# Another order for the same pieces of a two-layer graph kernel

## The chip, the cores and the metric

The kernel runs on one core of a Trainium2 chip. A core has five instruction queues that run at the same time: TensorE (PE, matrix products, with its weight loads shown as PEld), VectorE (DVE), ScalarE (ACT), GpSimd (POOL) and SyncE (SP, which issues the transfers here). Each works through its own instructions strictly in order and waits for the others by semaphores. The metric is device time in microseconds, lower is better.

## The reference

128 graphs of 128 nodes with 64 features pass two layers, each closed by a residual and a layer norm. In the first, every node j sums a ReLU over its neighbours k; in the second, a two-layer message is summed with the adjacency as weights and goes through a gated update.

```python
# layer 0, per graph: x [128, 64], adj [128, 128]
mask = (adj > 0.0)
h  = relu((x @ W1a)[:, None, :] + (x[:, None, :] - x[None, :, :]) @ W1b + b1)   # [j, k, 192]
hm = einsum('jkh,jk->jh', h, mask)
x  = layernorm(x + hm @ W2 + deg[:, None] * b2)
# layer 1
m   = relu(relu(x @ W1 + b1) @ W2 + b2)
msg = relu(adj @ m)
r, z = sigmoid(...), sigmoid(...)          # of msg @ W_ih and x @ W_hh, with biases
n   = tanh(i_n + r * h_n)
x   = layernorm(x + (1 - z) * n + z * x)
```

## The kernel before

The inner sum of layer 0 is ReLU(u_j + v_k), and ReLU(a) = (a + |a|) / 2, so the kernel sums absolute values over the neighbours. It does not go over all 128 k. The neighbours of a node are ranked in each half of the graph; for rank r a 0/1 matrix `pick` says which k is the r-th neighbour of each j. A product of `pick` with the rows of v (the *gather*, L628) fetches that neighbour's v for all nodes at once. The first eight ranks of each half come from `pick0` (comparisons of `rankT` with a constant, L534); nodes with more neighbours borrow extra rows, and `pick1` (comparisons of `place`) serves those with four more ranks. `own` and `past` (L480, L481) say which extra row belongs to which node: the *row owners* of the title's change, turned by PE (`pq`, L508) into `ownT` (L511).

The graphs are worked on in 32 groups of four. A group has 24 *stretches* (six for each graph: four with `pick0`, two with `pick1`), and a stretch takes two ranks of both halves:

- *seed* (L597, ACT): copy u four times into a PSUM buffer `pv`
- *gather* (L628, PE): 12 products add the picked v, which is held as three bfloat16 pieces `b0`, `b1`, `b2`
- *reduce* (L644, DVE): sum of absolute values of the buffer into `part`

There are three `pv` buffers, so the seed of stretch k+3 waits for the reduce of stretch k. All the rest must find a place between the stretches. To prepare a later group: masks (L428, POOL), ranks (L435, L438), degrees (L443 to L448), counts (L453 to L463, POOL), offsets with own/past, turned, places (L517 to L527), values (u and v: `pu` L544 and L547, `uv` L551), pieces (`b0` L563, `r` L566, `b1` L569, `b2` L572), the picks, over (`pz` L608, `us` L615: u of the extra rows). To finish a group: base (L656), together (sums of `part`, L666 to L673, POOL), sums (`ph` L685 and L686, `hmT` L692), second (`pw`, `y` L305 and the first layer norm L274 to L287, which gives `x1`), turn, message1 to 3 (`pm`, `pn`, `pa`), gates (`pg`, `rz` L366, `rh` L368, `n` L369) and update (tanh L374, four sums, second layer norm, store). All of these steps that use a product share two further PSUM buffers (the pool `ps_w`), taken in turn: a product waits until the result that lay in its buffer two takings before has been read out by ACT or DVE.

The order is written out by hand, as a timetable. Each part is a generator; one entry in its list of times is one step, up to the next `yield`. The times are in units of no meaning beyond their order; a group is `PER` units long, and group g runs the same list shifted by `g * PER`:

```python
for name, times in TIMETABLE.items():
    if g == 0 and name in FIRST:
        times = FIRST[name] + times[len(FIRST[name]) :]
    run = parts[name]()
    for t in times:
        plan.setdefault(g * PER + t, []).append(run)
...
with tc.manual_schedule():
    for t in sorted(plan):
        for run in plan[t]:
            next(run, None)
```

So the sorted times set the order of the instructions on every queue, and which of the two `ps_w` buffers a step gets. Nothing else is decided by them: what an instruction waits for is its operands and its buffer. In the steady state the work of one group's length contains stretches of group g, finishing of groups g-1 to g-5 and preparation of groups g+1 to g+3.

Of the kernel before, what the change touches and what calls it, by code (L numbers as in the profile page):

```python
# [26 lines left out]
EPS = 1e-5  # L27


PER = 768  # L30
TIMETABLE = {
    "load": (-1520,), "masks": (-559,), "ranks": (-122, -122), "degrees": (-402, -367), "turned": (-19, -1),
    "counts": (-114,), "offsets": (-22, -22, 80, 228, 245, 348, 349), "owners": (1039, 1066), "places": (368, 431),
    "pieces": (337, 538, 550, 595), "others": (1085, 1194), "values0": (-55, -50, -37), "values1": (204, 204, 268),
    "pick0": (-44, 50, 88, 133, 133, 137, 251, 419), "pick1": (663, 679, 679, 679), "over0": (578, 602),
    "over2": (1053, 1123), "base0": (693,), "together0": (728, 840, 1185, 1275), "sums0": (1392, 1392, 1405),
    "base1": (708,), "together1": (1189, 1219, 1289, 1289), "base2": (443,), "together2": (1345, 1353, 1370, 1370),
    "sums2": (1443, 1449, 1449), "base3": (717,), "together3": (1408, 1417, 1417, 1417),
    "second": (1425, 1453, 1473, 1502, 1502, 1503), "turn": (1504, 1504), "message1": (1512, 1512),
    "message2": (1534, 1538), "message3": (1539, 1696), "gates": (2002, 2032, 2052, 2068, 2068, 2080),  # L40
    "update": (2201, 2201, 2333, 2396, 2584, 2918, 3390, 3734, 4832),
    "seed": (644, 644, 657, 674, 684, 685, 711, 728, 728, 741, 761, 837, 923, 937, 978, 1149, 1149, 1173, 1203, 1221,
        1271, 1326, 1395, 1397),
    "gather": (661, 661, 681, 681, 686, 708, 730, 730, 737, 748, 767, 940, 1026, 1051, 1110, 1161, 1163, 1189, 1238,
        1317, 1338, 1405, 1405, 1405),
    "reduce": (664, 678, 684, 684, 706, 724, 740, 743, 780, 862, 894, 947, 1119, 1138, 1138, 1192, 1215, 1233, 1263,
        1358, 1358, 1407, 1407, 1407),
}


SETUP = (-8001, -7999, -7610, -7530, -7400, -7380, -700, -690)
FIRST = {
    "load": (-8000, -7998), "masks": (-7580,), "ranks": (-7520, -7515), "degrees": (-7389, -7388), "counts": (-7387,),
    "offsets": (-7372, -7371, -7366, -7366, -7366, -7366, -7365), "turned": (-7359, -7358),
    "values0": (-7375, -7374, -7370), "values1": (-7368, -7364, -7360), "pieces": (-7373, -7363, -7355, -7350),
    "places": (-7357, -7356), "pick0": (-7512, -7512, -7512, -7512, -7365, -7365, -7365, -7365),
    "pick1": (-7352, -7352, -7351, -7351), "over0": (-7349, -7348), "seed": (-7369, -7366, -7361, -7354),
    "gather": (-7367, -7362, -7354, -7351), "reduce": (-7365, -7358, -7353, -7350),
}

@with_exitstack
def adj_resnorm_kernel(  # L80
# [316 lines left out]
    with ExitStack() as fast:  # L397
# [323 lines left out]
        name, g, run = "setup", -1, setup(ps_g, ps_w)  # L721
        for t in SETUP:
            plan.setdefault(t, []).append(run)
        for g in range(ng):
# [9 lines left out]
            if g == ng - 1:  # L734
                plan.setdefault(g * PER + TIMETABLE["reduce"][-1] + 1, []).append(parts["spare"]())
            for name, times in TIMETABLE.items():
# [3 lines left out]
# [3 lines that stand above are left out]
# [126 lines left out]
```

## Time and profile before

| what | value |
|---|---|
| median of 3 runs (lowest to highest) | 1049.1 us (1049.07 to 1049.19) |
| span of the profiled execution (no other time of it is given) | 1047.0 us |
| first reduce of group 0 | 18.82 us |
| reduce 4 of group 0 | 33.08 us |
| `y` (L305) of the first, the 31st and the last group | 64.01, 996.04, 1023.81 us |
| `y` to `y` in an undisturbed middle group | 30.98 us |
| granted TensorE clock, mean | 0.983 (1.00 from 62 to 1000 us) |
| reduces: 768, busy | 699.6 us |
| comparisons: 384, busy | 120.5 us |

The span is the time from the first to the last instruction; the times measured without the profiler are a little longer than it. `y` is the instruction with which a finished group leaves the first layer; it occurs once for each group, so its distance is the length of a group. Busy time counts an instruction's whole length; successive instructions of one engine overlap at their ends, so the distance from start to start is shorter than the length (a reduce is recorded at 949 ns and follows the one before after 865).

### The profile page before, as it was taken

To read this page: it belongs to the slowest core of one execution; us is meant where nothing else is said; L and a number is where in the kernel's file an instruction comes from. 1 tells how busy PE (TensorE), PEld (TensorE's weight loads), DVE (VectorE), ACT (ScalarE), POOL (GpSimd) and SP (SyncE) were. 2 spreads that over 40 slices of the span, in tenths; PEclk is the share of its full clock that TensorE was granted. 3 is DMA by queue.
4 is the path that set the end of the run, shared out by engine and by line. 5 is a ranking of instruction groups with operands and counts; after the bars stand their busy time and mean duration, and the time that the engine had idled before them with its cause. 6 is when DMAs were issued, how large, how long until landed. Compare 5 with 4: busy or idle time off the path is not lost.

```text
span 1047.0 us, 33471 instructions
## 1 busy us (share of the span) xinstructions
PE 952.5 (91%) x13447; PEld 761.0 (73%) x13447; DVE 972.5 (93%) x2202; ACT 943.0 (90%) x1608; POOL 876.6 (84%) x1281
## 2 busy tenths in 40 slices
PE   6798999999999999999999999999999999999984
PEld 3577777777787777777777777777777777777762
DVE  6988999999999999999999999999999999999983
ACT  4789999999999999999999999999999999999971
POOL 2568788889888888988888988988898888898864
PEclk7899999999999999999999999999999999999997
DMA  4000000000000000000000000000000000000000
GB/s 111 1 23 2 23 21 23 28 27 10 19 27 27 27 27 27 3 27 28 26 28 28 4 24 28 27 28 28 24 5 28 27 27 27 27 3 7 7 8 28
DMA packets 21368, 23.95 MB, mean 23 GB/s; under 512 B 4050, under 2 KB 17112, under 8 KB 21208
## 3 DMA queue, kind: packets, MB, share of 16 engines
q1 hardware_dynamic: 21208, 21.76, 7.0%
q8 instruction: 107, 1.75, 0.7%
q14 instruction: 53, 0.43, 0.1%
HBM read 17.55 MB, written 4.19 MB: 21 GB/s over the span
## 4 chain that ended last, share of the span: by engine, by line
PE 31%; DVE 21%; ACT 20%; POOL 20%; issue 7%; DMA 0%; SPq 0%; DVEq 0%; POOLq 0%; ACTq 0%
PE pv L628 12%; ACT pv L597 10%; DVE part L644 10%; PE ph L686 3%; ACT uv L551 3%; POOL part L666 3%; PE pu L544 2%; POOL rs L281 2%; DVE stats L274 2%; DVE pick L534 2%; ACT b L563 2%; PE ph L685 2%; POOL part L670 2%; POOL part L673 2%; POOL r L566 2%
## 5 line engine op out<-in xcount | busy, mean ns | idle before, releaser
L644 DVE TENSOR_REDUCE part<-pv 128x192 f32<-128x768 f32 x768 | 699.6, 949 | 31.6 <-PE pv L628 15.6
L628 PE MATMUL pv<-b,pick 64*128 64x192 bf16 x9216 | 501.6, 244 | 39.1 <-ACT pv L597 34.9
L628 PEld LDWEIGHTS <-pick 64*128 64x128 bf16 x9216 | 385.0, 94 | 123.9 <-issue 94.4
L597 ACT COPY pv<-uv 128x768 f32<-128x768 f32 x512 | 407.5, 804 | 16.6 <-DVE part L644 14.2
L597 ACT COPY pv<-us 128x768 f32<-128x768 f32 x256 | 204.7, 817 | 13.2 <-DVE part L644 13.1
L666 POOL TENSOR_TENSOR part<-part 128x384 f32<-128x384 f32 x128 | 127.8, 998 | 19.7 <-DVE part L644 17.7
L551 ACT COPY uv<-pu 128x512 f32<-128x512 f32 x128 | 75.1, 587 | 27.3 <-PE pu L547 23.1
L544 PE MATMUL pu<-wall,xT 64*128 64x512 f32 x256 | 92.3, 637 | 1.4 <-ACT off L473 1.2
L534 DVE TENSOR_SCALAR pick<-rankT 128x512 bf16<-128x512 bf16 x256 | 88.6, 367 | 1.3 <-ACT rankT L438 1.3
L686 PE MATMUL ph<-ownT,part 128*96 128x128 f32 x512 | 87.6, 273 | 0.2 <-POOL part L673 0.2
L487 POOL CAST own<-own 128x512 f32<-128x512 bf16 x32 | 19.5, 610 | 75.2 <-DVE own L481 69.1
L668 POOL TENSOR_TENSOR part<-part 128x192 f32<-128x192 f32 x128 | 77.3, 604 | 5.1
L572 POOL TENSOR_TENSOR b<-r,b 128x1024 bf16<-128x1024 f32 (+1 forms) x35 | 68.8, 1966 | 12.1 <-ACT b L569 8.9
L670 POOL TENSOR_TENSOR part<-part 128x192 f32<-128x192 f32 x128 | 75.6, 590 | 2.6
L608 PE MATMUL pz<-uv,own 128*128 128x192 f32 x256 | 58.6, 352 | 20.4 <-DVE n L369 12.0
L300 PE MATMUL pw<-w2c,hmT 96*128 96x64 f32 x512 | 75.1, 278 | 0.7 <-ACT hmT L692 0.7
L673 POOL TENSOR_TENSOR part<-part 128x192 f32<-128x192 f32 x128 | 75.5, 590 | 0.0
L300 PEld LDWEIGHTS pw<-w2c,hmT 96*128 96x128 f32 x512 | 69.8, 192 | 6.8 <-issue 4.9
L686 PEld LDWEIGHTS ph<-ownT,part 128*96 128x96 f32 x512 | 70.9, 166 | 1.8 <-POOL part L673 0.7
L685 PE MATMUL ph<-ident,part 128*96 128x128 f32 x256 | 71.0, 277 | 0.8 <-POOL part L670 0.6
L281 POOL TENSOR_TENSOR rs<-ve,nhalf 128x4 f32<-128x4 f32 x64 | 66.7, 1042 | 5.3
L566 POOL TENSOR_TENSOR r<-uv,b 128x1024 f32<-128x1024 f32 x31 | 66.0, 2130 | 0.0
(148 smaller groups left out, 1588.4 us busy)
## 6 DMA issues: line engine op xcount, KB each, us to landing
adjT<-in_adjT_dram SPq DMA_DIRECT2D x32, 256.0 KB, 2.8
xT<-in_xT_dram SPq DMA_DIRECT2D x64, 64.0 KB, 2.6
x<-in_x_dram SPq DMA_DIRECT2D x32, 128.0 KB, 2.4
out_dram<-o SPq DMA_DIRECT2D x32, 128.0 KB, 2.0
wab<-in_w_dram SPq DMA_DIRECT2D x2, 96.0 KB, 2.5
bi<-in_b_ih_dram SPq DMA_DIRECT2D x1, 96.0 KB
bias<-in_b_hh_dram SPq DMA_DIRECT2D x1, 96.0 KB
wx<-in_w_hhT_dram SPq DMA_DIRECT2D x2, 48.0 KB, 3.6
```

The lines of the kernel that those rows point to most:

```text
L300: nc.tensor.matmul(p[:, i, :], s["hmT"][:, i, c, :], w2c[:, c, :], start=c == 0, stop=False)
L534: nc.vector.tensor_scalar(s[name][:, i], s[src], 2.0 * (first + i) - 1.0, None, ALU.is_equal)
L544: nc.tensor.matmul(ps[h], s["xT"][ks, i, :], wall[ks, :], start=True, stop=False)
L551: nc.scalar.copy(uv[:, 2 * h + i, :], ps[h])
L597: nc.scalar.copy(v, src.rearrange("p (c b h) -> p c b h", c=1, b=1).to_broadcast(list(v.shape)))
L628: nc.tensor.matmul(v[:, h, j, :], pick[ks, a + j, i, :], s[f"b{c}"][ks, i, F : F + H], start=False, stop=c == 2, skip_group_check=True,)
L644: nc.vector.tensor_reduce(into, view(s["pv", i, k]).rearrange("p c b h -> p h c b"), AX.XY, ALU.add, apply_absolute_value=True,)
L666: nc.gpsimd.tensor_tensor(f[:, 0:2], f[:, 0:2], f[:, 2:4], ALU.add)
L670: nc.gpsimd.tensor_tensor(f[:, 0], f[:, 0], f[:, no], ALU.subtract)
L673: nc.gpsimd.tensor_tensor(f[:, 0], f[:, 0], f[:, 1], ALU.add)
L685: nc.tensor.transpose(p[:, i, c, :], s["part", i0 + i][:, 0, cs], ident)
L686: nc.tensor.matmul(p[:, i, c, :], s["part1", i0 + i][:, 0, cs], s["ownT"][:, i0 + i, :], start=False, stop=True, skip_group_check=True,)
```

## The change

Only the two timetables, the list `SETUP` and the unit `PER` differ; every instruction is the same, and each queue has as many as before. The whole shift of the numbers (PER ten times as large, a later zero) means nothing; the order that comes out is what counts. Within a group's length, against the stretches:

- copies of u (seed) stand one stretch sooner on ACT relative to small results such as `m1`, `m2` and the first `uv` of values0, which come behind a further copy
- ranks: PE's product from before gather 0 to after gather 4
- row owners (`pq`): from after gather 12 to after gather 10
- message3: from after gather 10 to after gather 13; places before degrees; over0 after sums0 instead of ahead of it
- comparisons on DVE: before, `pick0` between reduce 5 and reduce 14 of the group ahead and `pick1` between reduce 23 and reduce 2; after, they stand behind reduce 14, 17, 20, 22, 23 and 0, `pick0` and `pick1` in mixed order, the last three of `pick0` only after the group's own reduce 0
- the statistics of update (L274): from after reduce 20 to after reduce 4
- `b0` (L563): from after seed 14 to after seed 17; the `base` rows are spread differently
- loads: two groups ahead instead of three
- the first group and the setup have their own order: the first adjacency load goes ahead of the weight loads, the load of group 1 behind all of setup's loads, degrees ahead of ranks, and seeds 4 and 5 ahead of the second group's ranks

```diff
-PER = 768
+PER = 7680
 TIMETABLE = {
-    "load": (-1520,), "masks": (-559,), "ranks": (-122, -122), "degrees": (-402, -367), "turned": (-19, -1),
-    "counts": (-114,), "offsets": (-22, -22, 80, 228, 245, 348, 349), "owners": (1039, 1066), "places": (368, 431),
-    "pieces": (337, 538, 550, 595), "others": (1085, 1194), "values0": (-55, -50, -37), "values1": (204, 204, 268),
-    "pick0": (-44, 50, 88, 133, 133, 137, 251, 419), "pick1": (663, 679, 679, 679), "over0": (578, 602),
+    "load": (-13730,), "masks": (-12008,), "ranks": (-5844, -5844), "degrees": (-10379, -10179),
+    "turned": (-4917, -4474), "counts": (-5544,), "offsets": (-5208, -5187, -4765, -4509, -3829, -3198, -1474),
+    "owners": (3311, 3746), "places": (-2998, -2655), "pieces": (-2359, -1040, -1012, -282), "others": (-2397, -1574),
+    "values0": (-5666, -5639, -5639), "values1": (-3673, -3446, -3378),
+    "pick0": (-2699, -2480, -1412, -657, -89, 643, 704, 916), "pick1": (-1456, -673, -79, 517), "over0": (-597, -272),
...
-    "seed": (644, 644, 657, 674, 684, 685, 711, 728, 728, 741, 761, 837, 923, 937, 978, 1149, 1149, 1173, 1203, 1221,
-        1271, 1326, 1395, 1397),
+    "seed": (-172, -168, 227, 921, 1341, 1368, 2018, 2018, 2445, 2612, 3169, 3460, 4084, 4145, 4425, 4839, 4956,
+        5224, 5461, 5704, 6457, 6732, 6776, 7296),
...
-    "reduce": (664, 678, 684, 684, 706, 724, 740, 743, 780, 862, 894, 947, 1119, 1138, 1138, 1192, 1215, 1233, 1263,
-        1358, 1358, 1407, 1407, 1407),
+    "reduce": (571, 936, 1241, 1588, 1982, 2334, 2334, 2605, 2916, 3415, 3415, 4224, 4224, 4511, 4736, 5225, 5348,
+        5582, 6391, 6623, 6925, 7255, 7423, 7607),
 }
-SETUP = (-8001, -7999, -7610, -7530, -7400, -7380, -700, -690)
+SETUP = (-113105, -109386, -107102, -104025, -100032, -97526, -25206, -11107)
 FIRST = {
-    "load": (-8000, -7998), "masks": (-7580,), "ranks": (-7520, -7515), "degrees": (-7389, -7388), "counts": (-7387,),
+    "load": (-113322, -99309), "masks": (-105433,), "ranks": (-95876, -94299), "degrees": (-101486, -100699),
+    "turned": (-92902, -92053), "counts": (-97744,),
...
```

## The prediction

> **What bounds the kernel now.** I read the page's busy shares first, then the chain of waits inside one middle group, then the timelines of that group on VectorE and GpSimd.
>
> ```profile
> PE 952.5 (91%) x13447; PEld 761.0 (73%) x13447; DVE 972.5 (93%) x2202; ACT 943.0 (90%) x1608; POOL 876.6 (84%) x1281
> ```
>
> No engine stands alone: three are over 90% busy. The first `y` (L305) comes at 64.0 us, the 31st at 996.0, so a group takes 31.07 us on average and 30.98 when nothing disturbs it. These lines of the chain of waits, cut to 590 to 626 us, show one such group from `y` to `y`:
>
> ```profile
> 592.14 0.43 DVE y L305
> ...
> 596.24 0.44 PE pt L312 x2
> ...
> 601.41 1.12 PE pu L544 x3
> 602.53 0.45 PE pu L547
> ...
> 612.17 0.30 DVE rh L368
> ...
> 612.93 0.89 PE pz L608 x4
> ...
> 623.12 0.43 DVE y L305
> ```
>
> The chain changes engine all the time. I cut the group at three VectorE points: `y` at 592.14, the gates' `rh` at 612.17, reduce 21 (stretch 21 of 24) at 615.84, the next `y` at 623.12. The pieces are A 20.03, B 3.67 and C 7.28, together 30.98 us. Next, VectorE's timeline, whose rows are start, length, instruction:
>
> ```profile
> 595.10 0.55 DVE L534 TENSOR_SCALAR pick<-rankT 128x512 bf16<-128x512 bf16 x1
> ...
> 598.27 0.56 DVE L534 TENSOR_SCALAR pick<-rankT 128x512 bf16<-128x512 bf16 x1
> ...
> 601.37 0.68 DVE L534 TENSOR_SCALAR pick<-rankT 128x512 bf16<-128x512 bf16 x3
> ...
> 608.22 3.75 DVE L644 TENSOR_REDUCE part<-pv 128x192 f32<-128x768 f32 x4 [0.42 <-PE pv L628]
> ```
>
> and GpSimd's beside it:
>
> ```profile
> 594.88 0.61 POOL L284 TENSOR_TENSOR yc<-y,mv 128x256 f32<-128x256 f32 x1
> ...
> 598.08 1.50 POOL L428 TENSOR_SCALAR maskT<-adjT 128x512 bf16<-128x512 f32 x1
> ...
> 601.41 0.48 POOL L279 TENSOR_SCALAR ve<-mv 128x4 f32<-128x4 f32 x1
> ```
>
> A comparison (`pick`) holds VectorE for 0.20 us when GpSimd works on 4-element rows (three in 0.68), but 0.47 when a large GpSimd instruction runs beside it (595.10: the next starts at 595.57). I call that a collision, price 0.27. Of twelve comparisons in this group two pay all of it and one (beside the mask's end) half: 0.7 us. None of those that read `place` pays: over 200 to 900 us they take 275 to 292 ns.
>
> **The change part by part.** Steady prices, as start-to-start distances when the engine does not wait: reduce 0.865, copy of u 0.73, 12 gather matmuls 0.60, `y` with its statistics 1.26, update's statistics 0.89, a `past`/`own` pair 0.55, degrees 0.15. From a reduce's start to the copy that reuses its buffer 0.99; copy to gather 0.85; gather to reduce 0.72. Times below count from `y`.
>
> *Piece A, PE's side.* Now update's statistics stand after reduce 4, so reduce 5 starts at 1.26+0.865+0.89 = 3.02, copy 8 at 4.01, gather 8 at 4.86 (`x1` arrives at 4.10, hidden). From there the new order leaves PE no wait. Gather 8 0.60, `pr` 0.33, `pm` 0.63, gathers 9 and 10 1.20, `pq` 0.33 (row owners, now two stretches sooner), `pn` 0.56, gather 11 0.60, `values1` 1.00, gathers 12 and 13 1.18, `pz` 0.87, `pa` 0.68, together 7.98. Gather 14 starts at 12.84 and reduce 14 at 13.56. Here lies the gain: before, `values1` waited for its second buffer and took 1.57 (1.12+0.45 above) instead of 1.00, because message3's result was released a copy too late; owners and message3 now stand where both buffers are free. Copies of u, a stretch sooner against the small results, delay none of them here: `m1` is ready at 7.5 and PE wants it at 7.95. The run goes on with gather 14 0.60, `ps` and `pd` 1.11, gathers 15 and 16 1.16, first gates 0.87, gather 17 0.60, second gates 0.68, and gather 18 starts at 17.86. Reduce 18 could start at 18.6 and `rh` at 19.5: A would win 0.55.
>
> *Piece A, VectorE's side.* Two comparisons now frame degrees after reduce 14, and two follow reduce 17. Reduce 14 ends at 14.43. By GpSimd's new order `x1` ends at 4.1 and the work behind it (0.95 + 1.47 + 1.35 + 0.55 + 0.95 + 0.55 + 0.55 + 0.69 + 0.55 + 0.57 + 0.55 + 0.58 + 0.55 + 0.69 + 0.57) fills it to 15.2, so both collide: 0.48+0.15+0.48, reduce 15 at 15.54, reduce 17 ends at 18.17. `r` (L566, 2.09) starts once the parts after reduce 15 are done, 17.4 to 19.4: two more collisions. Reduce 18 starts at 19.13, `rh` at 20.0: A stays at 20.0, the gain is given back.
>
> *Piece B.* Sums0 goes before over0: the same two jobs. 0.53 (`rh`, `n`) + 0.13 + 1.35 + 0.87 + 0.75 = 3.63: no change. The two comparisons between reduce 20 and 21 take the place of update's statistics (0.89) and are hidden by this; uncovered they cost 0.4 to 0.95.
>
> *Piece C.* VectorE sets it: seven reduces 6.06, and now six comparisons where four stood (before they and their small waits filled the 1.22 left). `pick0.4` pays 0.08, `pick1.2` 0.27 (beside `together3`, released by reduce 21), `pick1.3` falls into a gap, and `pick0.5` to `.7` after reduce 0 run beside `o`, `ub`, `uc`, which reduce 23 releases: 0.81. C is 6.06+1.22+1.16 = 8.45. PE, waiting at sums2 for GpSimd, would allow about 7.3.
>
> [...]
>
> *Other moves.* Pieces' first cast (`b0`) goes three copies later; `b2` then ends about 1.5 before gather 0 wants it; uncovered, up to 2.1 a group. Ranks go from before gather 0 to after gather 4; the first comparison is ten stretches away. The four `base` rows change places on ACT (0.36 each, same sum). GpSimd's counts stand before `ve` and leave it free 1.2 before `mv`. SP loads two groups ahead instead of three and behind a store; landing takes 2.8, the mask has about 5: nothing, uncovered up to 2.8 once, since SP's later loads keep that lead.
>
> *First group.* SP issues the first adjacency load before the weights (0.6 each way), degrees come first, the four early comparisons later. Reduce 0 comes at about 17.5 instead of 18.82. Copies 4 and 5 stood behind the second group's ranks (which wait for a mask until 30.5); now they stand ahead of them. Reduce 4 should start at 30 instead of 33.08: 3 us gained, bounds 0 and 5 (the idle VectorE rows before it). Group 1's load is issued after fourteen weight loads, about 16.5 instead of 6.83; its mask runs at 26 or later.
>
> *Tail.* From the last `y` at 1023.81 to 1047.0 the chain is one group's own and keeps its order: 0, bounds -1.5 and +1.5 (the longest wait in it that another group could set).
>
> Sum: a group 20.0+3.65+8.45 = 32.1, 1.1 more; 30 such groups +33, first group -3, and some groups will hide a little: +27. The span goes from 1047.0 to 1074. The page gives no other time for the profiled execution; the median lies 2.1 above its span, kept as what lies around it: 1076.
>
> **The rivals.**
> *The comparisons do not collide* (faster). If GpSimd's large rows stand elsewhere than I place them, A is 19.5, B 3.65, C 7.3: 30.4 a group, 30 x -0.55 - 3 = -19, 1030. For it: PE's waits for copies (34.9 us in 42 by the list of waits) and the late buffer of `values1` do vanish. Against: reduce 0 to reduce 1 has `o`, `ub`, `uc` beside it by its own release. It decides when fewer than some five of twelve collide on the path.
> *Half of them count.* Collisions in A are hidden behind PE, only C's remain: 19.5+3.65+8.45 = 31.6, or 31.2 with two of the trio free. Total 1052 to 1065. Nothing excludes it; A's two sides differ by 0.5.
> *More waits.* Copies ahead of the small results make ACT sit on a buffer while `uv`, `m1` or hmT are wanted; each costs up to 0.5 a group (ACT's longest steady wait for `values1` is 0.52). One of them makes 32.6 a group and 1095, two make 33.1 and 1110.
>
> **How the numbers follow.** Forecast (1066 to 1088) 0.45; half 0.22; no collisions 0.20; more waits 0.13. The range 1040 to 1094 leaves out about 0.1 below (most of the collision-free case) and 0.1 above. A measurement here can tell 0.2%, about 2 us: faster 0.20, same 0.03 (the half case's lower edge), slower 0.77.
>
> **What would show it.** `y` to `y` of 32.1 in the middle. Comparisons from `place` no longer 284 ns but some near 550, all comparisons together rising from 120 us to about 180. `values1` in 1.0 without a wait. A of 20.0, C near 8.4. Reduce 4 of the first group near 30. I am wrong if C stays near 7.3, or if PE waits inside its run from gather 8 to 18.

## The result, and the profile after

The changed kernel takes 1155.5 us (median of four runs, 1154.3 to 1156.8) against 1049.1 us for the kernel before, measured beside it. The ratio is 1.1009, with a 95% interval of 1.0993 to 1.1025. The profiled execution has a span of 1155.0 us, 108.0 us more than before.

One thing has to be known to read the rows. The timetable of the changed kernel is fifteen lines shorter, so every line number is 15 lower than before: the reduce is L629 (before L644), the gather L613 (L628), the copy of u L582 (L597), the comparison L519 (L534), `own` L466 (L481), `r` L551 (L566), `b2` L557 (L572), `y` L290 (L305), `n` L354 (L369), the parts L651 to L658 (L666 to L673), `ph` L670 and L671 (L685 and L686), `pz` L593 (L608). The experiments keep the line numbers of before, except where it is said.

The first two lines of the changed kernel's page that matter are the busy shares and the granted TensorE clock in forty slices:

```profile
PE 1025.6 (89%) x13446; PEld 816.3 (71%) x13447; DVE 1061.6 (92%) x2202; ACT 958.2 (83%) x1608; POOL 881.2 (76%) x1281
...
PEclk9999999999999989999899998999989999899998
```

VectorE is busy for 89 us more and TensorE for 73 us more, although both have the instructions that they had. So instructions have become longer. The clock line says why for TensorE: it no longer gets its full clock in the middle of the run (mean 0.943; before 0.983, and 1.00 from 62 to 1000 us). For VectorE the groups by line say it, whose last three columns are the busy sum in us, the mean length in ns, and idle time:

```profile
L519 DVE TENSOR_SCALAR pick<-rankT 128x512 bf16<-128x512 bf16 x256 | 123.7, 503 | 0.0
...
L519 DVE TENSOR_SCALAR pick<-place 128x512 bf16<-128x512 bf16 x128 | 85.5, 670 | 0.0
```

The comparisons of `rankT` had a mean of 367 ns, those of `place` 291. Together they rose from 120.5 us to 209.2.

The first `y` comes at 61.68 us (before 64.01), the last at 1133.21, and from there to the end it is 21.8 us (before 23.2). So the ends of the run gained 2.3 and 1.4 us, and the 31 distances between them lost 111.7. The loss is in the steady state. I cut each of the groups 5 to 25 at the three points of the prediction and took the mean. In the table, "blocked" is the length of the comparisons, `past` and `own` of a group over what they take when GpSimd leaves them alone (0.283, 0.245 and 0.351 us), and "half clock" the time in a group in which TensorE was granted half its clock.

| kernel | group | A (`y` to `rh`) | B (`rh` to reduce 21) | C (reduce 21 to `y`) | blocked | half clock |
|---|---|---|---|---|---|---|
| before | 31.00 | 20.03 | 3.67 | 7.30 | 0.70 | 0 |
| after | 34.98 | 21.37 | 5.33 | 8.28 | 4.19 | 4.27 |

The three pieces lost 1.34, 1.66 and 0.98 us. The VectorE timeline of one group in the middle, from `y` to `y`, shows where:

```profile
614.77 0.41 DVE L290 TENSOR_TENSOR y<-pw,t 128x256 f32<-128x256 f32 x1
...
624.30 0.73 DVE L466 SCALAR_TENSOR_TENSOR own<-iota,off,past 128x128 bf16<-128x128 bf16 x1
...
633.08 1.66 DVE L519 TENSOR_SCALAR pick<-place 128x512 bf16<-128x512 bf16 x1
634.66 0.68 DVE L519 TENSOR_SCALAR pick<-rankT 128x512 bf16<-128x512 bf16 x1
...
636.13 0.27 DVE L353 TENSOR_TENSOR rh<-rz,pg 128x128 f32<-128x128 f32 x1
...
641.34 1.82 DVE L629 TENSOR_REDUCE part<-pv 128x192 f32<-128x768 f32 x2 [1.97 <-PE pv L613]
...
645.78 1.31 DVE L519 TENSOR_SCALAR pick<-rankT 128x512 bf16<-128x512 bf16 x3
...
649.61 0.41 DVE L290 TENSOR_TENSOR y<-pw,t 128x256 f32<-128x256 f32 x1
```

and GpSimd's timeline beside it:

```profile
624.29 0.60 POOL L653 TENSOR_TENSOR part<-part 128x192 f32<-128x192 f32 x1
...
632.46 2.13 POOL L551 TENSOR_TENSOR r<-uv,b 128x1024 f32<-128x1024 f32 x1
634.55 0.64 POOL L653 TENSOR_TENSOR part<-part 128x192 f32<-128x192 f32 x1
...
645.97 0.77 POOL L365 TENSOR_TENSOR ub<-ua,rz 128x256 f32<-128x256 f32 x1
```

`pick1.0` starts at 633.08, 0.62 us into `r`, and lasts 1.66 us, until 634.74. `r` ended at 634.59. The next comparison stands beside the addition of 634.55 to 635.19 and ends at 635.34. Two comparisons that need 0.48 us alone have taken 2.2. In A this is the largest single loss; an `own` of 0.73 instead of 0.35 at 624.30 stands beside an addition in the same way, and the three comparisons at 645.78 stand beside `ub` and others in C.

What follows in B is on TensorE. Its timeline in the same group, with the idle time before an instruction and what ended it in brackets:

```profile
634.19 0.67 PE L613 MATMUL pv<-b,pick 64*128 64x192 bf16 x12 [0.34 <-ACT pv L582]
636.87 0.28 PE L670 MATMUL ph<-ident,part 128*96 128x128 f32 x1 [2.01 <-DVE n L354]
...
638.84 1.49 PE L593 MATMUL pz<-uv,own 128*128 128x192 f32 x4
640.26 1.96 PE L613 MATMUL pv<-b,pick 64*128 64x192 bf16 x36
```

sums0 stands ahead of over0 now. Its `ph` needs the `ps_w` buffer of the first gates, which is free when the first `n` has read it. In the kernel before, over0's `pz` had this place and the same wait, only shorter:

```profile
612.93 0.89 PE L608 MATMUL pz<-uv,own 128*128 128x192 f32 x4 [0.38 <-DVE n L369]
```

In both kernels the job behind gather 20 starts about 0.75 us after the first `rh` (612.93 after 612.17, and 636.87 after 636.13). So the order of the two jobs is not what made the difference. TensorE did its gathers in time, and the two comparisons made reduce 18 and the gates late: it has nothing to do for 2.0 us instead of 0.38. The busy time by windows shows what it does then (start and end, length, busy time of PE, PEld, DVE, ACT and POOL with counts, granted clock, DMA share, GB/s):

```profile
634.00:637.00 3.00, 0.80 (x14) 0.60 (x14) 2.93 (x7) 2.48 (x5) 2.92 (x4) 1.00 0.02 5
637.00:640.00 3.00, 3.00 (x16) 2.81 (x15) 2.37 (x5) 1.78 (x4) 1.49 (x2) 0.58 0.00 0
```

After three microseconds with 0.80 us of work the granted clock is 0.58 on average in the next three. The four products of `pz` take 1.49 us instead of the 0.89 of before, gather 21 comes late, and VectorE waits 1.97 us for it: the bracket at 641.34 above. The half-clock stretches last 3.41 us in most groups and 6.83 in every fourth.

### The profile page after: what moved, and what is told of

Its sections match the earlier page's. It is cut to its first block, busy times and chain, and to the rows that moved or that the text cites. A ratio compares the mean times of both kernels' runs of the same rounds, so it can differ in the third digit from the quotient of the medians.

```text
span 1155.0 us, 33471 instructions
## 1 busy us (share of the span) xinstructions
PE 1025.6 (89%) x13446; PEld 816.3 (71%) x13447; DVE 1061.6 (92%) x2202; ACT 958.2 (83%) x1608; POOL 881.2 (76%) x1281
## 3 DMA queue, kind: packets, MB, share of 16 engines
q8 instruction: 107, 1.75, 0.6%
HBM read 17.55 MB, written 4.19 MB: 19 GB/s over the span
## 5 line engine op out<-in xcount | busy, mean ns | idle before, releaser
L629 DVE TENSOR_REDUCE part<-pv 128x192 f32<-128x768 f32 x768 | 697.9, 945 | 62.5 <-PE pv L613 60.0
L613 PE MATMUL pv<-b,pick 64*128 64x192 bf16 x9216 | 523.7, 248 | 36.4 <-ACT pv L582 31.9
L613 PEld LDWEIGHTS <-pick 64*128 64x128 bf16 x9216 | 404.5, 96 | 137.7 <-issue 103.3
L582 ACT COPY pv<-uv 128x768 f32<-128x768 f32 x512 | 413.7, 817 | 77.8 <-DVE part L629 71.0
L582 ACT COPY pv<-us 128x768 f32<-128x768 f32 x256 | 207.8, 812 | 69.6 <-DVE part L629 65.2
L651 POOL TENSOR_TENSOR part<-part 128x384 f32<-128x384 f32 x128 | 127.6, 997 | 169.2 <-DVE part L629 166.8
L670 PE MATMUL ph<-ident,part 128*96 128x128 f32 x256 | 82.1, 321 | 58.1 <-DVE n L354 58.1
L519 DVE TENSOR_SCALAR pick<-rankT 128x512 bf16<-128x512 bf16 x256 | 123.7, 503 | 0.0
L671 PE MATMUL ph<-ownT,part 128*96 128x128 f32 x512 | 112.8, 321 | 0.2 <-POOL part L658 0.2
L529 PE MATMUL pu<-wall,xT 64*128 64x512 f32 x256 | 100.8, 655 | 1.4 <-ACT rank L488 0.6
L671 PEld LDWEIGHTS ph<-ownT,part 128*96 128x96 f32 x512 | 87.2, 201 | 3.6 <-POOL part L658 0.4
L670 PEld LDWEIGHTS ph<-ident,part 128*96 128x96 f32 x256 | 36.6, 143 | 69.5 <-POOL part L655 63.7
L519 DVE TENSOR_SCALAR pick<-place 128x512 bf16<-128x512 bf16 x128 | 85.5, 670 | 0.0
L557 POOL TENSOR_TENSOR b<-r,b 128x1024 bf16<-128x1024 f32 (+1 forms) x35 | 68.7, 1963 | 16.5 <-ACT b L554 16.5
L658 POOL TENSOR_TENSOR part<-part 128x192 f32<-128x192 f32 x128 | 78.3, 612 | 0.0
L593 PE MATMUL pz<-uv,own 128*128 128x192 f32 x256 | 71.0, 412 | 0.0
```

The costliest lines, as they stand in the source:

```text
L519: nc.vector.tensor_scalar(s[name][:, i], s[src], 2.0 * (first + i) - 1.0, None, ALU.is_equal)
L529: nc.tensor.matmul(ps[h], s["xT"][ks, i, :], wall[ks, :], start=True, stop=False)
L582: nc.scalar.copy(v, src.rearrange("p (c b h) -> p c b h", c=1, b=1).to_broadcast(list(v.shape)))
L613: nc.tensor.matmul(v[:, h, j, :], pick[ks, a + j, i, :], s[f"b{c}"][ks, i, F : F + H], start=False, stop=c == 2, skip_group_check=True,)
L629: nc.vector.tensor_reduce(into, view(s["pv", i, k]).rearrange("p c b h -> p h c b"), AX.XY, ALU.add, apply_absolute_value=True,)
L651: nc.gpsimd.tensor_tensor(f[:, 0:2], f[:, 0:2], f[:, 2:4], ALU.add)
```

## The experiments

My theory after the result had two parts. First, a comparison that meets a large GpSimd instruction stands still until that instruction ends, so the new places of the comparisons cost far more than the 0.27 us each that I had put down. Second, the wait that this makes on TensorE before sums0 halves its clock, and that is B's loss. The rivals were that the order of the small results and of the copies of u on ACT and TensorE is worse in itself, or that the half clock is only a sign of the loss.

**The disputed price alone.** A separate program computes nothing of the reference (its output is zeros). On VectorE a mark is written, then eight comparisons or six `own` rows follow, while GpSimd runs one instruction of the kernel's kinds that the mark releases.

```diff
+for what in ("none", "mask", "sub", "add", "cast"):
+    for kind in ("pick", "own"):
+        nc.vector.memset(marks(what), 1.0)   # releases GpSimd's instruction
+        pool(what)
+        nc.vector.memset(wait, 0.0)
+        ...                                  # 8 comparisons, or 6 own rows
```

> Leaves out the whole computation (the output is zeros): GpSimd runs one instruction (the mask, the subtraction of r over 128x1024, the addition of together over 128x384, the copy of own32) while VectorE runs eight comparisons or six own rows on other tiles. Theory, block: the first comparison that meets a GpSimd instruction with two SBUF inputs ends only when that instruction ends (about 1.5 to 2 us beside the subtraction, up to 0.9 beside the addition), later ones cost 0.20. Rival, fixed price as in the prediction: every comparison beside any large GpSimd instruction costs 0.47 and none more than 0.56. The mask row of before (a comparison of 0.56 inside a mask of 1.50) speaks for the rival, and the theory has to show the mask as another kind.

VectorE's timeline of this program: the eight comparisons beside the mask, beside a subtraction of the size of `r`, beside an addition of 384 elements, and beside nothing:

```profile
36.01 2.45 DVE L150 TENSOR_SCALAR pick<-rank 128x512 bf16<-128x512 bf16 x8
...
40.75 3.56 DVE L150 TENSOR_SCALAR pick<-rank 128x512 bf16<-128x512 bf16 x8
...
48.11 2.43 DVE L150 TENSOR_SCALAR pick<-rank 128x512 bf16<-128x512 bf16 x8
...
57.66 1.64 DVE L150 TENSOR_SCALAR pick<-rank 128x512 bf16<-128x512 bf16 x8
```

GpSimd's instructions beside the first three:

```profile
35.91 1.80 POOL L133 TENSOR_SCALAR maskT<-adj 128x512 bf16<-128x512 f32 x1 [4.98 <-DVE adj L145]
...
40.64 2.31 POOL L135 TENSOR_TENSOR big<-big,bigh 128x1024 f32<-128x1024 f32 x1 [0.41 <-DVE big L145]
...
47.99 1.19 POOL L137 TENSOR_TENSOR part<-part 128x384 f32<-128x384 f32 x1 [1.28 <-DVE part L145]
```

Beside the subtraction the second comparison takes 2199 ns and ends at 43.09; the subtraction ended at 42.95. Beside the addition one takes 1073 ns, ending 0.15 us behind it. After that the rest run at 280 ns. An `own` row is held up just as long (2196 and 1069 ns). The mask is another matter: of the comparisons beside its 1.80 us, two took 695 and 685 ns and two between them 280. The copy of 512 elements, with one input, holds a comparison too (689 ns beside its 0.81 us). So of the four kinds tried only the mask lets VectorE in between, and the row that spoke for a fixed price was a mask: in the kernel before, the comparison of 598.27 ended at 598.83 and the mask at 599.58.

**The two comparisons out of `r`.** In the changed kernel, `pick0.2` and `pick1.0` go from behind reduce 17 to the other two after reduce 14.

```diff
-"pick0": (-2699, -2480, -1412, -657, ...), "pick1": (-1456, -673, -79, 517)
+"pick0": (-2699, -2480, -2478, -657, ...), "pick1": (-2477, -673, -79, 517)
```

> The changed kernel, with only the two comparisons behind reduce 17 moved ahead of reduce 15, where GpSimd waits for that reduce. Theory, blocked comparison: nothing meets r any more, the gates come about 1.4 us sooner, TensorE does not idle 2 us before sums0 and keeps its full clock; A falls from 21.4 to about 20.2, B from 5.3 to about 3.8, a group from 35.0 to about 32.3, the total from 1155 to about 1070. Rival, order of the small results: A and B are long because copies of u stand ahead of small results; two comparisons are worth at most 1.4 us a group, the clock still falls, the total stays above 1110.

1090.6 us, ratio 1.0395 [1.0378, 1.0413]. A fell from 21.37 to 19.68, below that of the kernel before, and the half clock is gone from the middle (mean of the run 0.989). B did not return to 3.67: it is 4.64, since `r` and `b2` now run earlier and the next pair of comparisons, between reduces 20 and 21, meets `b2`. VectorE's row of this kernel:

```profile
604.35 1.34 DVE L534 TENSOR_SCALAR pick<-place 128x512 bf16<-128x512 bf16 x1
```

and GpSimd's, which ended at 605.54:

```profile
603.41 2.13 POOL L572 TENSOR_TENSOR b<-r,b 128x1024 bf16<-128x1024 f32 x1
```

The theory's direction holds and 65 us of the 106 came back with two instructions. Its size was short, because a collision that is taken away in one place lets GpSimd run ahead and makes another.

**Work for TensorE in its idle time.** Thirty products without use stand ahead of sums0, into the buffer of gather 20. With them the output is not the reference's; all other instructions and their order are the changed kernel's.

```diff
 # in gathers, after stretch 20's products
+if (i, k) == order[20] and s["g"] < ng - 1:
+    for _ in range(30):
+        nc.tensor.matmul(s["pv", i, k][:, 0, C * H : 512], ones_h, zeros[:, 0 : 512 - C * H], ...)
```

> The changed kernel with 30 products more on TensorE in each group between gather 20 and sums0 (into columns of the gather's buffer that nothing reads). They fill the idle 2 us and change no order. Theory, the clock falls because TensorE idles there: it stays full, B falls from 5.3 to about 4.0 while A stays at 21.4, the total falls by about 1.4 x 30 to some 1112. Rival, the clock falls for another reason (load, or whatever the new order does elsewhere): half clock remains in each group, more work makes it slower, 1155 to 1170.

1111.5 us, ratio 1.0600 [1.0582, 1.0618]. B went from 5.33 to 3.59, while A (21.37) and C (8.28) stayed as they were, and so did the blocked time (4.21). The half clock is gone (mean of the run 0.994). In the list of waits (engine, its line, what it waited for: us in all, times, longest) the wait for `n` went with it, since the thirty products now fill it; `ph` was L670 in the changed kernel,

```profile
PE ph L670 <- DVE n L354: 58.1, 30, 2.0
```

and is L691 here:

```profile
PE ph L691 <- DVE n L369: 6.5, 28, 0.3
```

Nothing was made earlier for TensorE, it was only kept busy, and the kernel got 44 us faster. So B's loss is the clock, and the clock falls because of the idle time. That rules out the half clock as a mere sign.

**The comparisons at before's places among the reduces.** In the changed kernel all twelve comparisons go back behind the reduces that they followed before; the rest stays.

```diff
-"pick0": (-2699, -2480, -1412, -657, -89, 643, 704, 916), "pick1": (-1456, -673, -79, 517)
+"pick0": (-5345, -4763, -4762, -4264, -4263, -4262, -3455, -2498), "pick1": (20, 940, 941, 942)
```

> The changed kernel with all twelve comparisons at the places that they had before (relative to the reduces); all else as changed. Theory, blocked comparisons carry the whole loss: a group of 30.5 to 31.2, total 1033 to 1055, clock full. Rival, the other moves (copies sooner, row owners, ranks, statistics, pieces later) lose time themselves: 32 or more a group, total above 1075.

1163.6 us, ratio 1.1093 [1.1075, 1.1112]: a miss, and the most useful one. By its total it lies where the rival had put it, so what speaks against the rival here is the blocked time alone; the run with small rows below separates the two. The blocked time rose to 4.47 us a group (comparisons 2.55, `past` 1.12, `own` 0.79). A is 23.46, B 3.60, C 7.92. The old places among the reduces are not the old places beside GpSimd, whose order is the new one. VectorE's rows in A and C of this kernel:

```profile
633.50 0.65 DVE L480 TENSOR_SCALAR past<-iota,off 128x128 bf16<-128x128 bf16 x1
634.18 0.75 DVE L481 SCALAR_TENSOR_TENSOR own<-iota,off,past 128x128 bf16<-128x128 bf16 x1
...
636.59 0.64 DVE L534 TENSOR_SCALAR pick<-rankT 128x512 bf16<-128x512 bf16 x1
...
653.07 1.66 DVE L534 TENSOR_SCALAR pick<-place 128x512 bf16<-128x512 bf16 x3
```

GpSimd's rows beside the second and the third of them:

```profile
634.05 0.73 POOL L377 TENSOR_TENSOR ua<-x,tn 128x256 f32<-128x256 f32 x1
...
636.46 0.61 POOL L492 TENSOR_TENSOR t<-uv,deg 128x256 f32<-128x256 f32 x1
```

Each of the two ends 0.15 or 0.16 us behind the GpSimd instruction that it meets. Much of the loss now comes from other instructions, and what decides is how the two queues lie against each other.

This run also shows the half clock, 0.68 us of it a group on average, where TensorE's longest idle time is only 1.28 us (windows with the columns of above; the granted clock is the third number from the end):

```profile
670.00:673.50 3.50, 1.73 (x28) 1.18 (x25) 3.46 (x6) 2.23 (x4) 3.28 (x7) 1.00 0.00 0
673.50:677.00 3.50, 3.12 (x35) 2.77 (x36) 3.38 (x7) 2.65 (x4) 1.15 (x2) 0.51 0.02 5
```

**All twelve beside small GpSimd rows.** Four comparisons each go beside `ve` and `rs` of the first layer norm (4 elements a row), beside those of the update, and beside the counts; the counts and update's step are moved to fit.

```diff
-"counts": (-5544,)
+"counts": (-7070,)
-"pick0": (-2699, -2480, -1412, -657, -89, 643, 704, 916), "pick1": (-1456, -673, -79, 517)
+"pick0": (-5612, -5611, -5610, -5609, -4763, -4762, -4761, -4760), "pick1": (940, 941, 942, 943)
-"update": (16874, 19863, 24871, 24871, 24871, 25105, ...)
+"update": (16874, 19863, 24871, 24871, 24871, 29970, ...)
```

> The changed kernel with the twelve comparisons placed where its GpSimd should work on 4-element rows: four behind reduce 4 (in place of update's statistics, which go back behind reduce 20), four behind reduce 8, four behind reduce 1 with the counts moved up beside them; all else as changed. Theory, blocked VectorE instructions (comparisons and own rows) carry the loss: blocked time falls from 4.2 us a group to about 1.0 to 1.5, a group takes 30.2 to 31.0, the total is 1025 to 1050. Rival, the other moves of the change lose time by themselves: 32 or more a group, above 1075, with little blocked time left.

1063.1 us, ratio 1.0115 [1.0089, 1.0140]: between the bands. No comparison is blocked any more (0.00 us a group). Two VectorE rows of this kernel, four comparisons in 0.89 us and an `own` that still meets an addition:

```profile
505.00 0.89 DVE L534 TENSOR_SCALAR pick<-rankT 128x512 bf16<-128x512 bf16 x4
...
513.67 0.73 DVE L481 SCALAR_TENSOR_TENSOR own<-iota,off,past 128x128 bf16<-128x128 bf16 x1
```

GpSimd's rows beside them:

```profile
504.87 1.06 POOL L281 TENSOR_TENSOR rs<-ve,nhalf 128x4 f32<-128x4 f32 x1
...
513.67 0.59 POOL L668 TENSOR_TENSOR part<-part 128x192 f32<-128x192 f32 x1
```

B and C are back at 3.60 and 7.28; A is 20.63, 0.6 above before, with 1.35 us of `past` and `own` still blocked. So 92 of the 106 us went with the places of the comparisons, the counts and update's statistics, without a change to the order of the copies of u, of the gathers or of the small results. No run separates the three; the statistics went back to where the kernel before has them.

**The reverse, in the kernel before.** One comparison, `pick1.0`, is put where `r` runs.

```diff
-"pick1": (663, 679, 679, 679)
+"pick1": (472, 679, 679, 679)
```

> The kernel before with one comparison in each group (the first that reads place) moved behind reduce 17, where GpSimd runs r; nothing else. Theory, a comparison there ends when r ends and the gates wait for it: blocked time rises from 0.7 to about 1.8 us a group, the group from 31.0 to 32.0 to 32.5, total 1080 to 1097; if TensorE's idle time before over0 grows beyond 1.5 us, half clock comes with it and the group takes up to 33.5 (1125). Rival, VectorE has slack there (it idled 0.42 and 0.19 us about reduce 18 before): at most 31.3 a group, 1049 to 1058.

1072.3 us, ratio 1.0213 [1.0195, 1.0231]. One instruction in another place costs 22.5 us against the kernel before, measured beside it. VectorE's row:

```profile
623.36 1.33 DVE L534 TENSOR_SCALAR pick<-place 128x512 bf16<-128x512 bf16 x1
```

and GpSimd's, which ended at 624.55:

```profile
622.41 2.14 POOL L566 TENSOR_TENSOR r<-uv,b 128x1024 f32<-128x1024 f32 x1
```

The blocked time rose by 1.04 us a group, and the group by 0.77: all of it in A. The clock stays full in these groups (mean of the run 0.988), with an idle time of TensorE of 1.15 us ahead of over0, so this is the price of the collision without the half clock. It is below the expected band, which had 1.0 to 1.5 us a group; 0.27 of the 1.04 us was hidden. The 1.5 us of idle time named there is no bound that a run shows: with before's places half the clock came with 1.28 us as the longest idle time.

**The first group's order in the kernel before.** `SETUP` and `FIRST` of the changed kernel, divided by ten, stand in the timetable of before.

```diff
-SETUP = (-8001, -7999, -7610, -7530, -7400, -7380, -700, -690)
+SETUP = (-11310.5, -10938.6, -10710.2, -10402.5, -10003.2, -9752.6, -2520.6, -1110.7)
-FIRST = {"load": (-8000, -7998), "masks": (-7580,), ...
+FIRST = {"load": (-11332.2, -9930.9), "masks": (-10543.3,), ...
```

> The kernel before with the changed setup and first-group times (divided by ten, as the unit is). In the profile of the changed kernel the first y comes 2.3 us sooner. If that is the first group's own order, the first y comes at about 62 here too and the total is 1046 to 1048; if it comes from the steady timetable (copies 4 and 5 ahead of the second group's ranks), the first y stays near 64 and the total within 1 us of before.

1047.76 us, ratio 0.9976 [0.9966, 0.9987]; the first `y` comes at 62.44 instead of 64.01, and a group is 31.02. So this part of the change is a gain of about 2 us (0.2%), and this version is a little faster than both kernels.

**Two tries on what is left.** Before still has 0.70 us of blocked comparisons a group. On top of the version above, three of them go to where GpSimd has small rows:

```diff
-"pick0": (-44, 50, 88, 133, ...)
+"pick0": (-58, -58, -58, 133, ...)
```

> The kernel before with the changed first group (as in the run e10) and its three blocked comparisons (pick0.0 to .2) moved between reduce 4 and 5, where GpSimd works on 4-element rows for the first layer norm. Theory: blocked time falls from 0.7 to about 0 a group; A is partly paced by TensorE, so 0.1 to 0.5 of it comes out: a group of 30.5 to 30.9, total 1032 to 1045. Rival, these comparisons were hidden beside TensorE's run anyway: 30.98 a group and the total of e10, 1046 to 1049.

1052.95 us, ratio 1.0032 [1.0020, 1.0044]: a miss. The blocked time halved to 0.35, and the group became longer, 31.25. The three comparisons delay reduce 5 by 0.62 us after `y`, and with it the seed that ACT copies next and the small results behind it, such as `off`; from reduce 14 on the group is 0.24 us behind the version above. VectorE's rows then show a wait that was not there, and another comparison that now meets GpSimd:

```profile
600.04 0.26 DVE L480 TENSOR_SCALAR past<-iota,off 128x128 bf16<-128x128 bf16 x1 [0.35 <-ACT off L473]
...
608.98 0.59 DVE L534 TENSOR_SCALAR pick<-rankT 128x512 bf16<-128x512 bf16 x1
```

The second try is on the 13 us by which the version with small rows is slower than before. Its first cast `b0` goes back ahead of three copies of u:

```diff
-"pieces": (-2359, -1040, -1012, -282)
+"pieces": (-2980, -1040, -1012, -282)
```

> The run e8 with one step more undone: the first cast of pieces (b0) goes back from behind seed 17 to before seed 15. In e8 VectorE waits 0.34 and 0.58 us before reduces 17 and 18 for copies that stand behind b0. Theory, b0's place costs that: A falls from 20.6 to 19.8 or 20.1, a group from 31.5 to 30.7 to 31.0, total 1037 to 1048. Rival, the own rows that GpSimd blocks (1.35 us a group) set A: no change, 1058 to 1066.

1065.9 us, ratio 1.0160 [1.0146, 1.0174], with A at 20.76: no gain. The place of `b0` is not what costs there. The blocked `past` and `own` rows (1.34 us a group) fit the size, but no run took them away alone, and in the version with small rows reduces 17 and 18 also wait 0.34 and 0.58 us for ACT. Which of the two makes the last half microsecond of a group stays open.

The steady groups of all versions, as means over the groups 5 to 25 in us:

| kernel | ratio | group | A | B | C | blocked | half clock |
|---|---|---|---|---|---|---|---|
| two out of `r` | 1.0395 | 32.58 | 19.68 | 4.64 | 8.26 | 3.88 | 0 |
| TensorE kept busy | 1.0600 | 33.24 | 21.37 | 3.59 | 8.28 | 4.21 | 0 |
| before's places | 1.1093 | 34.98 | 23.46 | 3.60 | 7.92 | 4.47 | 0.68 |
| small rows | 1.0115 | 31.51 | 20.63 | 3.60 | 7.28 | 1.35 | 0 |
| small rows, `b0` sooner | 1.0160 | 31.64 | 20.76 | 3.60 | 7.28 | 1.34 | 0 |
| before, one into `r` | 1.0213 | 31.77 | 20.80 | 3.67 | 7.30 | 1.74 | 0 |
| before, first group's order | 0.9976 | 31.02 | 20.05 | 3.69 | 7.28 | 0.68 | 0 |
| the same, three moved | 1.0032 | 31.25 | 20.28 | 3.69 | 7.28 | 0.35 | 0 |

## Why the prediction was wrong

The direction was right, and the size was not: +27 us was forecast and 106 came, far beyond the range. Two steps failed.

*The price of a collision, 0.27 us each.* It was read at 595.10, from a comparison that met only the last 0.39 us of `yc`, and used as a fixed price for `r`, for the additions and for all others. What it shows is the rest of a short instruction: the comparison (0.55 us) ended 0.16 us behind `yc` (594.88 for 0.61), just as the comparisons in the separate program end behind the instruction that they met (0.14 us behind the subtraction, 0.15 behind the addition). That row fits a fixed price and a wait to the end alike, and the mask's row (598.27) fits the fixed price alone; but the mask is the kind beside which comparisons of 280 ns went through in the separate program. The place was right: `pick1.0` was predicted to stand in `r`. There it waited 1.38 us (1.66 less 0.28), and not 0.27. So A was not 20.0 but 21.37.

*B, "Sums0 goes before over0: the same two jobs".* For the order of the two this was right: the first of them waits for `n` in both kernels. The step that failed is that the wait was taken to stay as it was. With `n` some 1.3 us late, TensorE had 2.0 us without work instead of 0.38, and the clock halved: B was 5.33 and not 3.65. The late `n` alone costs B nothing, as the run with TensorE kept busy shows (3.59 against 3.65 predicted). The prediction had no term for the clock at all, and none of its rivals did: "More waits" had the wait on ACT. This term is 1.74 us in a middle group and 44 us in all, by that run.

What held:

- C was put at 8.45 and came at 8.28. Its collisions are with GpSimd rows of 0.6 to 0.8 us, and there the small price did. In its parts this is luck: in the group shown `pick1.2` was to pay 0.27 and paid nothing, `pick1.3` was to fall into a gap and paid 0.19.
- PE's side of A was right. `values1` has no wait left (about 1.0 us), TensorE runs from gather 8 to 18 without one, and gather 18 starts 17.5 us after `y` in the group shown (17.86 predicted). With the two comparisons out of `r` A is 19.68, near the 19.5 that the prediction named as what TensorE would allow. The gain of the new order exists; the collisions eat it.
- The first group gained 2.3 us against 3 predicted: reduce 4 at 31.23 (30 predicted, 33.08 before), and reduce 0, put at 17.5, at 18.88 (18.82 before). But one profile does not fix these: over the eight profiles with the new first group, reduce 0 came at 17.26 to 18.91, reduce 4 at 29.93 to 32.07 and the first `y` at 59.81 to 63.24. All eight first `y` lie ahead of the two with the old order (64.01 and 64.52). The tail, put at 0, gained 1.4 us.
- All comparisons together, put at about 180 us, took 209.2, and those of `place`, put near 550 ns, took 670: the right sign with the wrong price. That `past` and `own` would be held up too (0.72 us a group) was not foreseen.

Of the rivals, the one with half of the collisions hidden was right in part. With the two comparisons out of `r`, 1.45 us a group are still blocked in A, and A is 19.68, so these are hidden beside TensorE. The two behind reduce 17 were not: with them A has 1.77 us more blocked and is 1.69 longer. And no rival had the clock. The collision-free rival (1030) was not reached even with no comparison blocked: that gave 1063.

## What to carry to other kernels

Where VectorE has comparisons or rows like `past` and `own` beside GpSimd work, an order has to be read on both queues at once: here the price of a meeting was what was left of the GpSimd instruction (a comparison took 2199 ns beside the subtraction of 2.31 us, 1073 beside the addition of 1.19), and it went by that instruction's kind (at most 695 ns beside the mask of 1.80), so take it from a row of the same kind or measure it alone. A wait that is moved onto TensorE can bring a second loss: behind the 2.0 us here came half the clock, and that was 1.74 us of B. Ask of each new wait whether the clock survives it. Moving instructions away from a collision shifts the other queue, so expect the next collision and look for it, or put them beside instructions that do not hold them, such as GpSimd's 4-element rows here (four comparisons in 0.89 us).

## What the runs showed of the hardware

- GpSimd's mask, one f32 input and a bfloat16 output, let VectorE's comparisons through (280 ns) for part of its 1.80 us; two others beside it took 695 and 685 ns. Its subtraction (2.31 us; a comparison beside it 2199 ns), its addition of 384 elements (1.19 us; 1073) and its copy of 512 elements (0.81 us; 689) did not.
- GpSimd rows of 4 elements did not hold VectorE's comparisons: four beside `rs` took 0.89 us, though `rs` runs for 1.06.
- GpSimd's instructions were longer too: in the separate program, where a VectorE fill and a comparison of 0.23 us overlap its start, the subtraction took 2.31 us (in the kernels 2.13) and the addition 1.19 (1.00).
- In the changed kernel's middle groups, with 2.0 us of idle TensorE once a group, the granted clock was halved for 3.41 or 6.83 us. In the run with before's places, where the longest idle time was 1.28 us with shorter ones beside it, it was halved for 0.68 us a group on average, while 1.15 us once a group (one comparison in `r`) left the clock full.
- Between 140 and 1000 us of the changed kernel TensorE was busy for 1.11 to 1.75 us in the 3.41 us, the length of the shorter half-clock stretch, ahead of each fall of the clock. In the run with before's places it was busy for 1.73 us in the 3.50 us ahead of the fall shown. In the kernel before, whose clock stayed full there, no 3.41 us between 100 and 900 us held less than 2.18 us of work. This is counted from the traces; no run varied it by itself.
